# Moving the units' operand sums and steps to other slots in a one-core Strassen kernel on Trainium2

## The chip, the cores and the metric

The kernel runs on one core of one Trainium2 chip. A core has five engines, each with its own instruction queue: TensorE (PE in the profile, with its weight loads as PEld), VectorE (DVE), ScalarE (ACT), GpSimd (POOL) and SyncE (SP), which here only starts DMA transfers. Engines run at the same time and wait for each other by semaphores; within an engine instructions run strictly in the order of its queue. The metric is device time in microseconds (us) of one execution; the runs shown with it are repeated executions of the same kernel.

## The reference

```python
def reference(x, W1, b1, W2, b2, init_h, gate_w, sgate_w, sup_w, sdown_w, rgate_w, rup_w, rdown_w):
    xn = layernorm(x)                        # x: 8 x 1024 x 512, float32
    hidden, forget, inp = split(xn @ W1 + b1, 3)          # W1: 512 x 3072
    diff = softplus(-forget) - softplus(-inp)
    log_coeffs, log_values = -softplus(diff), -softplus(-diff) + log_g(hidden)
    out_h = scan over the 1024 positions, in log space, from log_g(init_h)
    s = out_h @ W2 + b2                      # W2: 1024 x 512
    shared = (silu(xn @ sgate_w) * (xn @ sup_w)) @ sdown_w     # 512 -> 1024 -> 512
    logits = xn @ gate_w                     # 32 experts, the best one is taken
    xs = xn * sigmoid(max(logits))
    routed = the same kind of layer with the weights of each token's own expert
    return x + s * silu(shared + routed)
```

All is in float32. There are 8192 tokens.

## The kernel before

**Two stages.** In the first (0 to some 2787 us of the profile) the recurrent layer and the shared expert are computed, the tokens' experts are chosen, and a table is built of which token goes where. In the second (2787 to 4124 us) the 32 routed experts run one after the other.

**Chunks, jobs and slots.** The first stage goes through 16 chunks of 512 tokens. A chunk has 20 *jobs*: blocks of the projections f, i, h (of W1), g and u (of the shared expert). A job is a product by Strassen's scheme: seven products of sums of quarters in place of eight products of quarters. Each product is one *slot* of PE work (`multiply`, matmuls on L925; ACT evicts the results on L939 and L941, VectorE and POOL join them on L951). So a chunk has SC = 140 slots; a slot is 1.21 us in the profile (169 to 170 us for a chunk).

**A hand-written order.** The kernel is emitted in the order in which the queues are to hold it. `now` counts slots. `at(slot, fn, ...)` puts a step into a slot. In each slot the loop at the end emits first the slot's product, then the steps that were put there, and then as many steps of the generator `project_out` (named `fill`) as `due(now)` asks for. No scheduler moves anything afterwards, but an engine reaches an instruction when its queue is done with those ahead of it, so that work put into slot 78 may run later, and never ahead of its place in the queue.

**Units.** What a chunk c produced is multiplied by the second matrix during chunk c+1, in two *units*: half 0 is the recurrent output times W2, half 1 the shared expert's product times sdown_w. A unit is again one Strassen product with seven banks, in the order P1, P2, P4, P6, P5, P3, P7. In chunks 1 to 13 a unit is "deep": each of the seven is itself done by Strassen's scheme, 49 steps in all. Steps of half 0 are due from slot 3 on and spread over 62 slots, those of half 1 over the 74 slots after. For each deep step there is a product of four matmuls (L1406), and for each bank:

- *outer sums* s1 to s4 of the unit's input (`out_combine`, L1275), four instructions of 128x256 each. s1 and s3 run on POOL, s2 and s4 on VectorE. There is one tile for each of s1 to s4, so a sum of the next unit overwrites that of this one and waits until PE has read it.
- *inner sums* of the quarters of those (`inner_sum`, L1388) on POOL;
- *inner evictions*: results are taken out of the accumulator bank by VectorE (L1415, the sum with a kept part; L1330, with the bias, for half 0) or ACT (L1324). A product waits for the eviction of the product before it in its bank.
- `out_add` (L1344) on VectorE, which adds the banks up, and then a store.

The weights of the steps come in pieces by DMAs that SP starts, four steps to a piece. Chunks 0, 14 and 15 are not deep: there the products of a bank are whole (L1461), and the bank of 128x512 is copied out by ACT (L1324), or by VectorE with the bias (L1330).

**The slots of the outer sums.** Half 0's sums of chunk c lie in slots 134 to 139 of chunk c and in slots 3 to 21 of chunk c+1 (q4 in 8 to 11, q3 in 18 to 21); half 1's in slots 62 to 85 of chunk c+1. For chunk 15 there are slots of their own ("fast").

**Ranks and table.** A step generator, `Dispatch.ranks`, counts for a quarter of the tokens how many before each chose the same expert. It runs one `yield` a slot (`spread_out`): VectorE makes one-hot rows and running sums, then it waits some slots, `aligned()` waits for the next group of seven slots, and two matmuls and a product and a sum on VectorE end it. It starts in slot 94 of chunks 2, 6 and 10. The fourth is the first part of `table()`, which starts in slot 77 of chunk 14 and goes on with `places` and `slots` (small VectorE operations on 128x64 tiles and 32-row columns, L1654 to L1691, and matmuls, L1606), `enter` (64 times, writes of rows to memory), `collect` and `merge`. The end of the table is the later of its own time and `END + 1`; both before and after, `END + 1` is the later.

**The tail.** After the last slot (END = 16 SC + 18) the rest of the last units runs alone, with the steps that are still open. In the sixth turn of that loop ACT starts the four DMAs of the first routed expert's first weights (`weight(0)`, `e_w`, L209); these stand in ACT's queue ahead of what is emitted later.

Of the kernel before, what the change touches and what calls it, by code (L numbers as in the profile page):

```python
# [34 lines left out]
def tile_kernel(  # L35
# [45 lines left out]
    nc = tc.nc  # L81
# [3 lines left out]
    E, _, I = rgate_w.shape  # L85
# [4 lines left out]
    NCHUNK = N // T  # L90
# [18 lines left out]
    def work(name):  # L109
        if now < SC:  # L110
            return pools["work"].tile([P, 512], FP, tag="w", name=name)
        assert now % 7 == 6
        return ps_x.tile([P, 512], FP, tag=f"x{(now // 7 + 1) % 2}", name=name)

    def aligned():
        while now % 7 != 6:
            yield
# [466 lines left out]
    def at(slot, what, *args):  # L584
        assert slot >= now
        steps.setdefault(slot, []).append(lambda: what(*args))
# [690 lines left out]
    for c in range(NCHUNK):  # L1277
        g = SC * (c + 1)
        fast = c == NCHUNK - 1
        for p in range(NP):  # L1280
            for q in range(1, 5):
                ends = p == NP - 1
                slot = {
                    1: 3 if ends else 134 + p - SC, 2: 6 if ends else 137 + p - SC,
                    4: 8 + p, 3: 13 + p // 2 if fast else 18 + p,
                }[q]
                at(g + slot, out_combine, c, 0, q, p)
                if fast:
                    slot = (24, 26, 31, 28)[q - 1] + p // 2
                else:  # L1290
                    slot = (62, 66, 82, 72)[q - 1] + p
                at(g + slot, out_combine, c, 1, q, p)

    def out_store(b, m, n):
# [25 lines left out]
    def out_copy(b, o, ps, first, n, reps=None):  # L1320

        c, half, name = ALL[b]
        if half or name not in ("P2", "P4", "P5"):
            nc.scalar.copy(o, ps)  # L1324
            return
        first += HC * (name == "P5")
        bias = b2b[:, first : first + n]
        if reps:
            bias = bias.unsqueeze(1).to_broadcast([P, reps, n])
        nc.vector.tensor_tensor(o, ps, bias, ALU.add)  # L1330
# [66 lines left out]
    def inner_product(step):  # L1397

        b, name = inner_of[step]
        if name == "P1":  # L1400
            out_bank[b] = out_bank_of(b)
        n = {"P2": 1, "P5": 2, "P3": 2}.get(name, 0)
        ps = out_bank[b][:, n * P : (n + 1) * P]
        w = out_w.pop(step)
        for i, lhs in enumerate(inner_lhs(b, name)):
            nc.tensor.matmul(  # L1406
                ps, lhsT=lhs, rhs=w[:, i, :], start=(name == "P1" and i == 0), stop=(i == 1),
                skip_group_check=True,
            )
        o = {"P2": (0, 0), "P3": (0, 1), "P4": (1, 0), "P7": (1, 1)}.get(name)  # L1410
        o = o and target(b)[:, o[0], o[1] * HQ : (o[1] + 1) * HQ]
        side = {"P2": "P1", "P3": "P6", "P7": "P5"}.get(name)
        if side:
            kept = inner.pop((b, side))
            nc.vector.tensor_tensor(o, ps, kept, ALU.add)  # L1415
        elif name == "P4":
            out_copy(b, o, ps, 0, HQ)
            at(now + 2, out_add, b)
        else:
            e = inner[b, name] = jp.tile(  # L1420
                [P, HQ], FP, tag="e" + name, name=f"e{name}_{b}", bufs=1 + (name == "P5")
            )
            out_copy(b, e, ps, 0 if name == "P1" else HQ, HQ)

    def project_out():
# [11 lines left out]
        for b, (c, half, name) in enumerate(ALL):  # L1437
# [14 lines left out]
            for q in range(2):  # L1452
                for p in range(NP):
# [17 lines left out]
                    if q == 1 and p == NP - 1:  # L1471
                        out_copy(
                            b, target(b), ps.rearrange("p (q f) -> p q f", q=2), 0, HC, 2
                        )
                        at(now + 1, out_add, b)
                        out_w.pop(("whole", b))
                        out_fetch()
                        if c == 0:
                            out_fetch()
# [8 lines left out]
    class Dispatch:  # L1488
# [16 lines left out]
        def ranks(self, q):  # L1505

            G = self.G
            q *= G
            oh = self.big([P, G, E], f"ohd{q}")
            nc.vector.tensor_tensor(  # L1510
                oh, self.bc(emax[:, q : q + G], E), self.rep(desc, G), ALU.is_equal
            )

            prev = self.big([P, G, E], f"prev{q}")
            yield
            if self.run is None:
                nc.vector.memset(prev[:, 0, :], 0.0)
            else:
                nc.vector.tensor_copy(prev[:, 0, :], self.run)
            for i in range(1, G):  # L1520
                nc.vector.tensor_tensor(
                    prev[:, i, :], prev[:, i - 1, :], oh[:, i - 1, :], ALU.add
                )
                if i % 4 == 3:
                    yield
            self.run = sm.tile([P, E], FP, name=f"run{q}", tag="run")
            nc.vector.tensor_tensor(self.run, prev[:, G - 1, :], oh[:, G - 1, :], ALU.add)
            for _ in range(9):
                yield
            yield from aligned()  # L1530
            ps = work(f"bef{q}")
            nc.tensor.matmul(
                ps, lhsT=upper, rhs=oh.rearrange("p t e -> p (t e)"), start=True, stop=False
            )
            nc.tensor.matmul(
                ps, lhsT=ones, rhs=prev.rearrange("p t e -> p (t e)"), start=False, stop=True
            )
            nc.vector.tensor_tensor(
                prev, ps.rearrange("p (t e) -> p t e", t=G), oh, ALU.mult
            )  # L1540
            yield
            nc.vector.tensor_reduce(rank[:, q : q + G], prev, AX.X, ALU.add)
            for _ in range(4):
                yield
            if q + G == NTILE:
                yield from aligned()
                self.totals = work("cps")
                nc.tensor.matmul(
                    self.totals[:, :E], lhsT=ones, rhs=self.run, start=True, stop=True
                )  # L1550
                nc.tensor.matmul(
                    self.totals[:E, E : E + 1], lhsT=self.run, rhs=ones[:, :1],
                    start=True, stop=True,
                )
# [267 lines left out]
    def due(slot):  # L1822

        c, s = divmod(slot, SC)
        if c == 0:
            return 0
        s -= 1
        before, (a, b) = sum(PER[: 2 * (c - 1)]), PER[2 * (c - 1) : 2 * c]
        if c == NCHUNK:
            return int(before + min(max(RATE * s, 0), a + b))  # L1830
        return int(before + min(max(s / 62, 0), 1) * a + min(max((s - 62) / 74, 0), 1) * b)
# [3 lines left out]
    for now in range(END):  # L1835
        job = now // 7
        name, back = ORDER[now % 7]
        if now < 7 * NPL:
            plain(job, now % 7)
        todo = (job - back,) if name != "P3" else (job - 1, job)  # L1840
        for n in todo:
            late = name == "P3" and n < JC
            if NPL <= n < NJOB and n == job - (1 if late else back):
                multiply(name, n)
        for step in steps.pop(now, ()):
            step()
        while filled < due(now):
            next(fill)
            filled += 1
# [21 lines left out]
    while filled < TOTAL:  # L1871
        now += 1
        for step in steps.pop(now, ()):
            step()
        while filled < due(now):
            next(fill)
            filled += 1
        k += 1
        if k in (6, 22):
            chunks[0].weight((0, "d")[k // 20], nc.scalar)  # L1880
        if filled >= TOTAL - 24 and "xsT" not in vars(chunks[0]):
            for t in range(CT):
                chunks[0].transpose(t)
# [143 lines left out]
```

## Time and profile before

| | us |
|---|---|
| runs | 4142.73, 4143.5, 4148.38 |
| median | 4143.5 |
| the profiled execution, its own time | 4148.08 |
| span of that execution | 4146.4 |
| mean granted clock of TensorE | 0.996 |

What PE did, and what stood ahead of the waits, by group of instructions in the profile:

| line, engine, what | count | busy us | idle before, us |
|---|---|---|---|
| L925 PE, the jobs' products (largest group) | 2536 | 654.6 | 11.1 |
| L1406 PE, deep steps from inner sums | 2912 | 445.5 | 22.2 |
| L1406 PEld, deep steps from outer sums | 1248 | 187.8 | 26.4 |
| L339 PE, the routed experts' second product | 2048 | 514.8 | 0.0 |
| L1388 POOL, inner sums of 128x256 | 208 | 221.1 | 99.8 |

How to read it: "busy" is the time of the group's instructions; "idle before" is the time in which their engine did nothing directly ahead of them, and the profile names what it takes to have ended that idle time, from the semaphores (the "releaser"). Where the named engine had long been done, it was another. Matmuls are pipelined, and PE is busy nearly everywhere: an idle stretch on PE is time lost, one on another engine is not unless PE waits for what comes late. The granted clock is the share of full speed at which PE was allowed to run.

The page divides the span into 40 slices. In the first 27 (the first stage) VectorE is busy 6 or 7 tenths and ACT 5 to 7; in the last 13 (the routed experts) PE is at 9 tenths of a slice or more and ACT at 2.

### The profile page before, as it was taken

The page shows a single profiled execution, that of the slowest core. Times are in us where ns is not written, and L with a number is a line of the kernel's source. Part 1 is how long each engine was busy: PE and PEld are TensorE (multiplying, and loading weights), DVE is VectorE, ACT ScalarE, POOL GpSimd, SP SyncE. Part 2 cuts the span into 40 slices and gives each one's busy share as a digit, 9 for nine tenths or more (in the row PEclk, how much of TensorE's full clock was granted, in tenths as well). Part 3 has the DMA queues.
Part 4 walks back from the last instruction along what each step waited for, and adds up shares of the span by engine and source line. Part 5 has one row for each costly group of instructions (what it writes and reads, how often), then busy time and mean ns, then how long its engine had stood idle before and what let it go on. Part 6 is the DMA issues. An engine that isn't in the chain of part 4 may idle for free. (4 is left out here: it accounts for less than half of the span.)

```text
span 4146.4 us, 70185 instructions
## 1 busy us (share of the span) xinstructions
PE 4059.2 (98%) x23699; PEld 3646.8 (88%) x23699; DVE 2642.8 (64%) x4489; ACT 2201.5 (53%) x4582; POOL 2254.1 (54%) x2603
## 2 busy tenths in 40 slices
PE   8999999999999999999999999999999999999997
PEld 6788889888888888988988888887899999999997
DVE  6766676676776766667676687444556656666631
ACT  5777766776667667676677765731222222222210
POOL 5445565555655655556655564634555555565542
PEclk9999999999999999999999999999999999999999
DMA  8788787787877778778777776666778788888884
GB/s 275 257 277 277 232 257 252 250 256 239 262 243 245 252 253 257 249 235 259 255 248 249 238 252 201 186 214 203 211 227 231 222 243 231 245 250 237 247 259 116
DMA packets 731387, 994.43 MB, mean 240 GB/s; under 512 B 75468, under 2 KB 523884, under 8 KB 730772
## 3 DMA queue, kind: packets, MB, share of 16 engines
q1 hardware_dynamic: 682020, 896.52, 67.8%
q0 software_dynamic: 46880, 89.20, 8.7%
q8 instruction: 193, 3.16, 0.3%
q10 hardware_dynamic: 2128, 4.19, 0.3%
q14 instruction: 166, 1.36, 0.1%
HBM read 858.39 MB, written 149.21 MB: 243 GB/s over the span
## 5 line engine op out<-in xcount | busy, mean ns | idle before, releaser
L925 PE MATMUL b<-t,sums 128*128 128x256 f32 x2536 | 654.6, 381 | 11.1 <-ACT u L939 5.2
L339 PE MATMUL acc<-e_h,e_wd 128*128 128x284 f32 (+26 forms) x2048 | 514.8, 394 | 0.0
L925 PEld LDWEIGHTS b<-t,sums 128*128 128x128 f32 x2536 | 455.4, 191 | 62.1 <-ACT u L939 7.3
L1406 PEld LDWEIGHTS u<-w_pieces,i 128*128 128x128 f32 x2912 | 435.7, 191 | 72.8 <-POOL i L1388 31.3
L1406 PE MATMUL u<-w_pieces,i 128*128 128x128 f32 x2912 | 445.5, 276 | 22.2 <-POOL i L1388 16.0
L339 PEld LDWEIGHTS acc<-e_h,e_wd 128*128 128x128 f32 x2048 | 373.8, 190 | 64.7
L260 POOL DMA_INDIRECT e_xs<-rec,fours x276 | 300.2, 1088 | 91.7 <-issue 88.6
L925 PE MATMUL b<-t,nat 128*128 128x256 f32 x1268 | 327.4, 381 | 4.7 <-ACT u L939 2.5
L925 PE MATMUL c<-t,sums 128*128 128x256 f32 x1268 | 328.3, 382 | 1.9 <-DVE lgT L694 1.5
L925 PE MATMUL c<-xnT,sums 128*128 128x256 f32 x1268 | 327.1, 381 | 2.4 <-ACT p L939 2.4
L925 PE MATMUL b<-xnT,nat 128*128 128x256 f32 x1268 | 327.5, 381 | 2.0 <-ACT i L941 2.0
L925 PE MATMUL a<-xnT,nat 128*128 128x256 f32 x1268 | 326.8, 380 | 0.0
L302 POOL COPY pin<-e_h 1x1 f32<-1x1 f32 x148 | 37.8, 255 | 479.3 <-DVE e_h L447 350.3
L1388 POOL TENSOR_TENSOR i<-s 128x256 f32<-128x256 f32 x208 | 221.1, 1065 | 99.8 <-PE u L1406 77.4
L941 ACT ACTIVATE u<-b,vec 128x256 f32<-128x256 f32 x378 | 180.5, 478 | 175.2 <-PE b L925 169.5
L925 PEld LDWEIGHTS b<-xnT,nat 128*128 128x128 f32 x1268 | 225.8, 191 | 37.4 <-DMA w_pieces<-d_P 7.8
L925 PEld LDWEIGHTS b<-t,nat 128*128 128x128 f32 x1268 | 228.0, 191 | 31.2 <-ACT u L941 4.2
L925 PEld LDWEIGHTS c<-t,sums 128*128 128x128 f32 x1268 | 225.6, 191 | 30.0 <-DVE lgT L694 7.2
L925 PEld LDWEIGHTS c<-xnT,sums 128*128 128x128 f32 x1268 | 226.8, 191 | 28.0 <-ACT p L939 4.9
L925 PEld LDWEIGHTS a<-xnT,nat 128*128 128x128 f32 x1268 | 226.7, 191 | 22.8
L1406 PEld LDWEIGHTS u<-w_pieces,s 128*128 128x128 f32 x1248 | 187.8, 191 | 26.4 <-DVE o L1415 10.1
L414 ACT COPY e_s<-e_b 128x284 f32<-128x284 f32 (+21 forms) x216 | 84.2, 390 | 237.3 <-PE e_b L405 237.3
(328 smaller groups left out, 9569.9 us busy)
## 6 DMA issues: line engine op xcount, KB each, us to landing
w_pieces<-d_P SPq DMA_DIRECT2D x1274, 128.0 KB, 3.2
sums<-sdram SPq DMA_DIRECT2D x300, 512.0 KB, 5.1
nat<-in_L_attn_W_dram SPq DMA_DIRECT2D x192, 512.0 KB, 4.7
e_w<-L_ffn_routed_gate_w_dram SPq DMA_DIRECT2D x126, 512.0 KB, 4.7
e_w<-n_L_ffn_routed_up_w_dram SPq DMA_DIRECT2D x126, 512.0 KB, 8.2
e_wd<-L_ffn_routed_down_w_dram SPq DMA_DIRECT2D x31, 2048.0 KB, 10.4
nat<-L_ffn_shared_gate_w_dram SPq DMA_DIRECT2D x64, 512.0 KB, 4.2
nat<-n_L_ffn_shared_up_w_dram SPq DMA_DIRECT2D x64, 512.0 KB, 4.2
```

The source lines that it names most:

```text
L260: nc.gpsimd.indirect_dma_start(out=self.xs[t][:, b, :], out_offset=None, in_=rec1.rearrange("n (a d) -> (n a) d", a=NA), in_offset=bass.In ...
L302: nc.gpsimd.tensor_copy(pin, self.mark)
L339: nc.tensor.matmul(accs[m][:, :W], lhsT=self.wd[:, j, m * P : (m + 1) * P], rhs=h[:, :W], start=(j == 0), stop=(j == NI - 1),)
L414: nc.scalar.copy(o[:, :W], ps[:, :W])
L925: nc.tensor.matmul(ps, lhsT=lhs[:, k, :], rhs=rhs[:, k, :], start=(new and k == 0), stop=(k == KQ - 1),  skip_group_check=True,)
L941: nc.scalar.activation(o, ps, AF.Identity, bias=bias(n, block))
L1388: nc.gpsimd.tensor_tensor(o, l, r, what)
L1406: nc.tensor.matmul(ps, lhsT=lhs, rhs=w[:, i, :], start=(name == "P1" and i == 0), stop=(i == 1), skip_group_check=True,)
```

## The change

Four edits, all of place and order but the last:

1. Half 1's outer sums of chunks 0 to 14: with p = 0 to 3, the slots of q1 (POOL) go from 62 + p to 68 + 2p, of q2 (VectorE) from 66 + p to 70 + 2p, of q3 (POOL) from 82 + p to 84 + 2p, and of q4 (VectorE) from 72 + p to 76 + 2p.
2. `due`: steps of the units begin two slots later in each chunk. All that a step emits goes along: products, inner sums, evictions, weight pieces, additions and stores. Half 0's outer sums stay in their slots.
3. `ranks`: the wait before its matmuls is 3 yields in place of 9, that at its end one in place of 4.
4. In the last unit (chunk 15, half 1) VectorE copies the banks out, not ACT.

```diff
@@ -1288,7 +1288,7 @@
                 if fast:
                     slot = (24, 26, 31, 28)[q - 1] + p // 2
                 else:
-                    slot = (62, 66, 82, 72)[q - 1] + p
+                    slot = (68, 70, 84, 76)[q - 1] + 2 * p
                 at(g + slot, out_combine, c, 1, q, p)
@@ -1321,7 +1321,10 @@
         c, half, name = ALL[b]
         if half or name not in ("P2", "P4", "P5"):
-            nc.scalar.copy(o, ps)
+            if c == NCHUNK - 1 and half:
+                nc.vector.tensor_copy(o, ps)
+            else:
+                nc.scalar.copy(o, ps)
             return
@@ -1525,7 +1528,7 @@
             nc.vector.tensor_tensor(self.run, prev[:, G - 1, :], oh[:, G - 1, :], ALU.add)
-            for _ in range(9):
+            for _ in range(3):
                 yield
             yield from aligned()
             ps = work(f"bef{q}")
@@ -1540,8 +1543,7 @@
             yield
             nc.vector.tensor_reduce(rank[:, q : q + G], prev, AX.X, ALU.add)
-            for _ in range(4):
-                yield
+            yield
             if q + G == NTILE:
                 yield from aligned()
@@ -1824,7 +1826,7 @@
         c, s = divmod(slot, SC)
         if c == 0:
             return 0
-        s -= 1
+        s -= 3
         before, (a, b) = sum(PER[: 2 * (c - 1)]), PER[2 * (c - 1) : 2 * c]
         if c == NCHUNK:
             return int(before + min(max(RATE * s, 0), a + b))
```

## The prediction

> **What bounds the kernel now.** I read the page first, then TensorE's waits by stretch, then timelines where the longest waits lie.
>
> ```profile
> span 4146.4 us, 70185 instructions
> PE 4059.2 (98%) x23699; PEld 3646.8 (88%) x23699; DVE 2642.8 (64%) x4489; ACT 2201.5 (53%) x4582; POOL 2254.1 (54%) x2603
> ```
>
> PE is busy 98% of the span. The change removes no matmul, so it can gain only what PE waits for, plus what PE loses at a low clock. The waits, first for the steady chunks (346 to 2381 us), then for the last chunks and the tail up to the routed experts (2381 to 2830):
>
> ```profile
> PE u L1406 <- POOL i L1388: 14.8, 13, 1.3
> PE u L1406 <- issue: 4.8, 12, 0.4
> PE u L1406 <- DVE o L1415: 2.5, 6, 0.4
> ...
> PE u L1406 <- DVE o L1415: 4.3, 2, 3.6
> PE u L1461 <- ACT T L1324: 1.7, 1, 1.7
> PE u L1406 <- POOL i L1388: 1.2, 1, 1.2
> PE u L1461 <- DVE h L1036: 1.1, 1, 1.1
> ```
>
> The columns are total us, times and longest. Units carry nearly all of it. Everything in these two answers, the 0.7 of the table's matmuls (L1606) and 0.4 of "issue" included, sums to 31.5 us. That caps the gain, clock aside.
>
> The largest row comes back once per chunk, every 169 to 170 us (438.50, 609.64, 778.66, ...): at 1.21 us per slot, slot 78 of 140. In chunk 4:
>
> ```profile
> 773.94 1.50 DVE L1072 TENSOR_TENSOR sh<-ssig,u 128x1024 f32<-128x1024 f32 x1
> 775.36 1.27 DVE L1275 TENSOR_TENSOR s<-sh,s 128x256 f32<-128x256 f32 x2
> 776.56 0.94 DVE L1344 TENSOR_TENSOR o<-o,o 128x512 f32<-128x512 f32 x1
> 777.53 0.83 DVE L1344 TENSOR_TENSOR o<-o,R 128x512 f32<-128x512 f32 x1
> 778.28 0.28 DVE L1415 TENSOR_TENSOR T<-u,eP 128x128 f32<-128x128 f32 x1
> 778.63 0.52 PEld L1406 LDWEIGHTS u<-w_pieces,i 128*128 128x128 f32 x4 [1.60 <-POOL i L1388]
> 778.66 0.68 PE L1406 MATMUL u<-w_pieces,i 128*128 128x128 f32 x4 [1.23 <-POOL i L1388]
> ```
>
> The profile blames POOL's inner sums (L1388), but POOL had made this product's operand long before. The product needs its bank, and the eviction `T<-u,eP` empties it at 778.56, 0.07 us before PE starts to load. Its own matmul ended near 772: the eviction stood six us in VectorE's queue. VectorE is the bound of this stretch alone:
>
> ```profile
> 764.00:780.00 16.00, 14.77 (x89) 12.02 (x87) 15.90 (x25) 7.51 (x20) 9.43 (x11) 1.00 0.66 217
> 780.00:796.00 16.00, 15.99 (x92) 14.35 (x92) 8.94 (x21) 14.16 (x28) 10.15 (x17) 1.00 0.89 280
> ...
> 2562.00:2564.00 2.00, 0.00 (x0) 0.00 (x0) 1.97 (x4) 0.00 (x0) 1.67 (x2) 0.81 0.06 23
> 2564.00:2566.00 2.00, 1.18 (x5) 1.18 (x6) 2.00 (x3) 0.00 (x0) 1.97 (x3) 0.50 0.01 0
> ```
>
> (Length; busy PE, PEld, DVE, ACT, POOL; granted clock.) DVE is busy 15.90 of 16.00 us, then 8.94. The two lower rows are the start of chunk 15, where PE stands 3.60 us and resumes at half clock.
>
> **The change, part by part.**
>
> *A: shared sums spread.* 16 sums of 128x256 per chunk, 15 chunks, no DMA. VectorE's q2 go from slots 66-69 to 70, 72, 74, 76, and q4 from 72-75 to 76-82; POOL's q1 from 62-65 to 68-74, q3 from 82-85 to 84-90. In the instruction order, six of the eight VectorE sums stood ahead of the late eviction; now three do. At 0.55 us each (4.53 us for eight in 764:780) three less are 1.7 us. *B: units two slots later* moves every PE step of the units, its inner sums, evictions and weight DMAs on SP by 2.42 us against sums and jobs, so PE asks 2.42 us later. Together 4.1 us of margin against waits of 1.0 to 1.3: all go. POOL's sums now run beside VectorE's, which costs something:
>
> ```profile
> L1275 DVE TENSOR_TENSOR s<-s,h x64: 390/416/951, 167.5 to 2739.2; 128x256 f32<-128x256 f32 x64
> L1275 DVE TENSOR_TENSOR s<-sh,s x64: 407/420/945, 265.5 to 2770.8; 128x256 f32<-128x256 f32 x64
> ```
>
> (min/median/max ns.) Alone 0.42, at worst 0.95: the three sums and two additions left ahead of the eviction could lose 0.5 each, 2.5 of the 4.1 us, and 1.6 still cover 1.3. I take -14.8-1.2 = **-16.0**; bounds -16.0 and -8.0 (half of the stretches stay late, or shift to another slot).
>
> This row speaks against A. [...] Taken as one engine at a time, four POOL sums of 0.72 would take 2.9 of the 4.1 us and leave about half of the waits: 4130 in place of 4122. The measured 0.95 shows the contention; no row here shows a full stop.
>
> B also acts at chunk starts: six waits of 0.42 at slot 8.6, behind evictions in VectorE's queue, against 2.42 us: **-2.5** (bounds -2.5, 0). The twelve 0.4 us "issue" waits are a late eviction too, at slot 40, where the whole unit moves with its evictions past other work: **0** (bounds -4.8, 0). Two half-0 sums (q4, slots 8-11) stay put and meet a tile that PE frees two slots later: rival R2. Here I take 0: VectorE ran the one at 863.86, and PE's read, ended by 861.71, moves to 864.1, so VectorE waits 0.3 at most. POOL's half-0 q1 sums (slots 134-136) wait two slots longer too, but the inner sums queued behind them are asked for two slots later: 0. SP's weight pieces (128 KB, 3.2 us to landing) keep their lead over the products, both moving together: 0.
>
> *C: shorter waits in the ranks.* Six and three yields less: the ranks' matmuls come a slot group earlier (chunk 2, 6, 10: slot 104), and the table's places, slots and row writes 7 slots, 8.5 us; the table's end is held by a fixed slot. The ranks' VectorE work was done in slot 101.7, so PE finds it ready: 0. In 2546 to 2561 VectorE is busy 14.59 of 15.00 us, some 7 us of it small table operations (L1654 to L1691); about 4.1 of them lie after 2550, just ahead of the late evictions. They leave; with B's 2.42 the margin is 6.5 us against 3.6 and 0.7 (2546.0): **-4.3**, and with the 3.6 goes the slow clock: 0.50 from 2564.8 to 2570, 5.2 us at half speed, **-2.6**. Bounds -6.9 and 0; the L1606 wait 0 (bounds -0.7, 0).
>
> *D: last unit's copies.* Seven 128x512 copies go from ACT (0.58) to VectorE (0.69 at L1330): seven times 0.11, in a stretch where each PE bank takes 3.4 us. They hide behind PE except the last: **+0.1** (bounds 0, +0.8).
>
> *E: the tail.* B's price. ACT issues expert 0's first weights at a fixed step, and was held there by a queue:
>
> ```profile
> 2755.16 0.58 ACT L1324 COPY o<-u 128x512 f32<-128x512 f32 x1 [6.32 <-PE u L1461]
> 2763.03 2.22 ACTq L209 DMA_DIRECT2D e_w<-L_ffn_routed_gate_w_dram  x2
> 2765.42 1.03 ACTq L209 DMA_DIRECT2D e_w<-n_L_ffn_routed_up_w_dram  x2
> 2766.55 0.58 ACT L1324 COPY T<-u 128x512 f32<-128x512 f32 x1 [10.81 <-DMA e_w<-L_ffn_routed_gate_w_dram]
> ```
>
> Behind these four issues stood one copy of half 0 (P7's bank), for which PE waited 1.71 us at 2767.19. With the unit five steps later two stand there, P3's and P7's. P3's bank is wanted eight steps earlier, eight times 0.43 us before 2765.5, so at 2762.0; its copy would end at 2765.1 (ACT freed 2 us sooner, as the table's DMAs go earlier) to 2767.1. PE waits 3.1 to 5.1 in place of 1.7: I take +2.1. D doesn't help: the copies that are held are half 0's, still ACT's. The 3.60 us row was followed by half clock, 2.6 us: +2.6. Two slots' later start ends the 1.10 us wait for the last scan at 2734.57: -1.1. **+3.6** (bounds -2.8, if ACT is freed in time, and +6.2, with 5.1 us and no gain at the scan).
>
> [...] This trace has the drop after 3.60 and nothing between that and 1.71.
>
> **Sum**: -16.0 -2.5 -4.3 -2.6 +0.1 +3.6 = -21.7, against the profiled 4148.1: 4126.4. That execution lies 4.6 above the runs' median, so 4143.5 - 21.7 = **4122**.
>
> **Rivals.**
> - *R1, the jam only moves.* For: DVE 15.90 of 16, POOL's sums now beside it, evictions' slack elsewhere only tenths. Against: 8.94 of 16 in the next stretch, where q4's tail now falls. Half of A, no B, half of the chunk 15 part: -8.0 - 3.4 + 3.6 + 0.1 = -7.7: 4136.
> - *R2, slower: half-0 sums collide.* They stay in their slots while PE frees their tile 2.42 us later. Where VectorE reaches q4 less than two slots late, it stands at the head of its queue until PE has read, up to 2.42 us, with evictions and job additions behind it, and PE waits for those. In 13 chunks 13 x 2.42 = +31: 4122 + 31 = 4153. For: at 863.86 against 864.1 there is no margin left, and whatever VectorE gains it waits. Against: VectorE is jammed from 848 to 868 whatever the shared sums do, and now never waits for PE there. It decides once VectorE catches up by more than the half us or so that evictions can be late.
> - *R3, the last chunks gain nothing.* The 3.6 us wait stays, since scans and additions of 1.2 to 1.8 us (L1036, L1072) stand right ahead of that eviction, and the tail is dear: -16.0 - 2.5 + 6.2 + 0.1 = -12.2: 4131.
> - *The change doesn't move what it says:* the table's end doesn't move, as said; nothing else is held so.
>
> **How the numbers follow.** 0.2% is 8.3 us, the least that this kernel's measurement tells from no change: 4135.2 to 4151.8 is "same". Forecast 0.60 (faster), R3 0.13 (faster), R1 0.15 (on the border; 0.14 same), R2 0.12 (slower). Faster 0.74, same 0.14, slower 0.12. Low end: all lower bounds, -16.0-2.5-4.8-6.9-0.7-2.8 = -33.7: 4110. High end: all upper bounds, -8.0+6.2+0.8 = -1.0: 4142.5, and a collision of 0.2 us in each of 13 chunks: 4145. R2's full price is left out.
>
> **What would show it.** A, B right: PE's wait on L1388 falls from 14 times to three or fewer, and DVE's busy time in slots 66 to 79 is clearly under 15.9 of 16. C: no idle over 1 us and no granted 0.50 at chunk 15's start. E: PE idle of 3 us or more near 2760 before L1461, ended by an ACT copy, two copies behind `e_w` issues. R2: idle over 1 us on DVE before L1275 with PE's L1406 as releaser, in most chunks. I am wrong if slot 78 still waits, if new waits of 0.3 us or more appear in most chunks elsewhere, or if the tail grows by more than 6 us.

## The result and the profile after

| | median, us | runs |
|---|---|---|
| before | 4143.5 | 7, from 4142.68 to 4148.38 |
| after | 4159.15 | 7, from 4158.43 to 4164.98 |

The changed kernel is slower: ratio 1.0037, 95% interval 1.0027 to 1.0047, or +15.65 us at the medians. 4122 had been forecast. The executions that are profiled from here on are each compared with the run that has VectorE's copies alone (4143.9 us in its profile, the same as before in its median), since the profiled execution of before was one of its slowest.

The page of the changed kernel:

```profile
span 4156.6 us, 70101 instructions
PE 4060.6 (98%) x23699; PEld 3650.5 (88%) x23699; DVE 2694.5 (65%) x4496; ACT 2204.5 (53%) x4575; POOL 2327.7 (56%) x2603
```

POOL has the same 2603 instructions as before and is busy 73.6 us longer. VectorE has seven more (the copies, 4.8 us) and is busy 51.7 us longer. So the same work takes both engines longer. The waits of TensorE, first the steady chunks (346 to 2381 us), then the last chunks and the tail (to 2830); line numbers are three higher after the inserted lines, so L1409 is the L1406 of before:

```profile
PE c L925 <- DVE lgT L694: 13.9, 12, 1.2
PE b L925 <- DVE t L837: 6.3, 6, 1.1
PE u L1409 <- DVE o L1418: 5.4, 11, 0.8
PE u L1409 <- POOL i L1391: 2.1, 6, 0.4
PE u L1409 <- POOL f L951: 1.8, 1, 1.8
...
PE u L1464 <- DMA w_whole<-tdram: 4.1, 1, 4.1
PE u L1464 <- ACT o L1327: 2.4, 1, 2.4
PE u L1409 <- DVE o L1418: 2.1, 2, 1.6
```

The waits of slot 78 and the 4.8 of "issue" are gone. In their place stand 13.9 us for `lgT`, the reduced logits of the router, once a chunk, and 11.7 us at the chunk starts, in the rows of `t` (L837, a sum of quarters of the chunk's input, which the jobs' products multiply) and of `o` (evictions). Chunk 4 at slots 76 to 80, the same place that the prediction showed of before:

```profile
775.82 1.21 DVE L1347 TENSOR_TENSOR o<-o,o 128x512 f32<-128x512 f32 x1
777.07 0.83 DVE L1347 TENSOR_TENSOR o<-o,R 128x512 f32<-128x512 f32 x1
778.41 0.28 DVE L1418 TENSOR_TENSOR T<-u,eP 128x128 f32<-128x128 f32 x1
778.61 0.67 DVE L694 TENSOR_REDUCE lgT<-lgt 128x128 f32<-128x512 f32 x1
779.34 0.92 PE L925 MATMUL c<-t,sums 128*128 128x256 f32 x3 [1.16 <-DVE lgT L694]
```

The late eviction `T<-u,eP` no longer holds PE. But right behind it in VectorE's queue stands the first reduction of the router's logits (L694). Its operand lies in the accumulator bank that the job's next product `c` needs, so PE waits 1.16 us there, at slot 79. The same two in the trace of before:

```profile
779.49 0.68 DVE L694 TENSOR_REDUCE lgT<-lgt 128x128 f32<-128x512 f32 x1
780.22 1.13 PE L925 MATMUL c<-t,sums 128*128 128x256 f32 x4
```

There the reduction ended at 780.17 and the product before `c` at 780.21, so PE lost nothing: the wait of 1.23 us just ahead, at slot 78, had covered this one.

By stage (starts of the same job's product in both traces, slot 25 of chunks 2, 14 and 15, and the start of the routed experts' second products):

| us | to chunk 2 | 12 chunks | chunks 14 to 15 | tail | rest |
|---|---|---|---|---|---|
| copies alone (as before) | 369.2 | 2036.0 | 180.6 | 211.3 | 1345.1 |
| after | 369.9 | 2044.1 | 177.3 | 220.2 | 1345.2 |

So +8.1 in the steady chunks, -3.3 in the last two, +8.9 in the tail. The first column varies by several us between runs of the same start (363 to 374 over all kernels here), and nothing is read from it.

### The profile page after: what moved, and what is told of

Read it like the earlier page. It is cut to its first block, busy times and chain, and to the rows that moved or that the text cites. A ratio compares the mean times of both kernels' runs of the same rounds, so it can differ in the third digit from the quotient of the medians.

```text
span 4156.6 us, 70101 instructions
## 1 busy us (share of the span) xinstructions
PE 4060.6 (98%) x23699; PEld 3650.5 (88%) x23699; DVE 2694.5 (65%) x4496; ACT 2204.5 (53%) x4575; POOL 2327.7 (56%) x2603
## 5 line engine op out<-in xcount | busy, mean ns | idle before, releaser
L1409 PEld LDWEIGHTS u<-w_pieces,i 128*128 128x128 f32 x2912 | 435.9, 191 | 58.8 <-POOL i L1391 10.9
L1409 PE MATMUL u<-w_pieces,i 128*128 128x128 f32 x2912 | 445.6, 276 | 6.1 <-POOL i L1391 2.1
L1275 POOL TENSOR_TENSOR s<-h 128x256 f32<-128x256 f32 x128 | 137.0, 1086 | 171.3 <-DVE h L1036 97.8
L1391 POOL TENSOR_TENSOR i<-s 128x256 f32<-128x256 f32 x208 | 188.1, 907 | 73.8 <-PE u L1409 71.2
L1409 PEld LDWEIGHTS u<-w_pieces,s 128*128 128x128 f32 x1248 | 186.2, 191 | 29.6 <-DVE o L1418 12.7
```

What stands on the lines that cost most here:

```text
L1275: eng.tensor_tensor(o, l, r, op_)
L1391: nc.gpsimd.tensor_tensor(o, l, r, what)
L1409: nc.tensor.matmul(ps, lhsT=lhs, rhs=w[:, i, :], start=(name == "P1" and i == 0), stop=(i == 1), skip_group_check=True,)
```

## The experiments

Differences are against the median of before that was measured with each kernel (4144.4 to 4145.8).

### Each part alone

The spread of the sums:

```diff
-                    slot = (62, 66, 82, 72)[q - 1] + p
+                    slot = (68, 70, 84, 76)[q - 1] + 2 * p
```

> Before with the spread of half 1's outer sums alone. Theory 1 (VectorE's jam has two deadlines, the eviction at slot 78 and the logits' first reduction at slot 79, and POOL's sums beside VectorE's take back most of what is moved away): PE still waits about 1.2 us at slot 78 in each chunk, the time is within 4 us of before (4143.5). Theory 2 (POOL's sums beside VectorE's are themselves the cost of the whole change): 8 to 15 us slower.

4143.08, **-1.4** (ratio 0.9996, interval 0.9987 to 1.0006). The wait of slot 78 stays; its row has 12.6 us in 13 waits against 14.8, and in chunk 4 it is 0.94 in place of 1.23. Theory 1.

The units two slots later, in `due`:

```diff
-        s -= 1
+        s -= 3
```

> Before with the units begun two slots later alone. Theory 1 (the later start brings the losses at the chunk starts, because half 0's sums stay in their slots and POOL stands longer ahead of them): PE waits at slots 9 to 13 of the chunks rise by about 1 us a chunk, the wait of slot 78 becomes one for the logits' reduction, chunk 15 keeps some 1.2 of its 3.6 us without the low clock; in the tail two copies behind the expert's weights, but no wait for a weight transfer: +4 to +14 us. Theory 2 (the sums' spread is the cost, the later start is gain): 0 to -8 us.

4163.06, **+18.6** (1.0027 to 1.0060). The 12 chunks take 2049.3 us, 13.3 more, and the tail 217.3, 6.0 more. PE's waits are 12.2 us for `lgT`, 6.3 for `t` and 9.5 for evictions and inner sums. This is theory 1, above its range: this edit alone loses more than the whole change.

The shorter waits in the ranks (the first yields 3 for 9, the last 1 for 4):

```diff
-            for _ in range(9):
+            for _ in range(3):
...
-            for _ in range(4):
-                yield
+            yield
```

> Before with the shorter waits in the ranks alone. Theory 1 (the table's small operations made chunk 15's eviction late; the tail is dear only where the table's transfer and the later weight transfers meet in SP's queue): -4 to -8 us, no PE wait over 1 us and no low clock at the start of chunk 15, no wait for a weight transfer over 1 us in the tail. Rival (the scans ahead of the eviction make it late, or the table's transfer blocks SP's queue by itself): 0 to +7 us.

4140.79, **-3.7** (0.9982 to 1.0001). Waits of PE in the last chunks fall from 3.6 and 0.7 to 1.1 and 0.2, and no transfer is waited for in the tail. This is theory 1's picture of the waits, the time a little short of its range; the interval just reaches no change.

VectorE's copies:

```diff
-            nc.scalar.copy(o, ps)
+            if c == NCHUNK - 1 and half:
+                nc.vector.tensor_copy(o, ps)
+            else:
+                nc.scalar.copy(o, ps)
```

> Before with the last unit's seven copies on VectorE alone. Both theories: within 1 us of before. Rival (VectorE's additions of half 0 stand ahead of the copies and PE waits for banks): +2 to +5 us in the tail.

4144.35, **-0.1** (0.9991 to 1.0010). As expected.

### POOL's sums beside VectorE's

The spread for VectorE's sums only; POOL's q1 and q3 stay at 62 to 65 and 82 to 85:

```diff
-                    slot = (62, 66, 82, 72)[q - 1] + p
+                    slot = (62 + p, 70 + 2 * p, 82 + p, 76 + 2 * p)[q - 1]
```

> Before, with VectorE's sums of half 1 spread as in the change (q2 70 to 76, q4 76 to 82) and POOL's left at their old slots (q1 62 to 65, q3 82 to 85). If POOL's sums beside VectorE's are what took the gain back: three sums of 0.55 less ahead of the eviction, PE's wait at slot 78 falls from 1.2 to below 0.3 us, 10 to 16 us less than before. If the spread sums would gain nothing anyhow: the wait stays at 0.9 to 1.2, within 3 us of before.

4121.68, **-22.8** (0.9929 to 0.9962), more than expected; no wait at slot 78 or 79 is left in the steady chunks. The only difference to the spread as a whole is where eight POOL instructions a chunk stand. VectorE runs the same list in the same order in both, so the timelines of chunk 4 can be laid side by side. First with the whole spread:

```profile
766.12 1.49 DVE L1068 TENSOR_TENSOR ssig<-ssig,g 128x1024 f32<-128x1024 f32 x1
767.54 0.67 DVE L1275 TENSOR_TENSOR s<-s,sh 128x256 f32<-128x256 f32 x1
768.13 0.67 DVE L951 TENSOR_TENSOR i<-c,u 128x256 f32<-128x256 f32 x1
768.73 0.28 DVE L1415 TENSOR_TENSOR R<-u,eP 128x128 f32<-128x128 f32 x1
768.93 1.55 DVE L1036 TENSOR_TENSOR_SCAN h<-i,ginit,f 128x512 f32<-128x512 f32 x1
...
774.60 0.28 DVE L1415 TENSOR_TENSOR T<-u,eP 128x128 f32<-128x128 f32 x1
```

and with POOL's sums left out of the stretch:

```profile
761.62 1.23 DVE L1068 TENSOR_TENSOR ssig<-ssig,g 128x1024 f32<-128x1024 f32 x1
762.76 0.42 DVE L1275 TENSOR_TENSOR s<-s,sh 128x256 f32<-128x256 f32 x1
763.10 0.42 DVE L951 TENSOR_TENSOR i<-c,u 128x256 f32<-128x256 f32 x1
763.43 0.28 DVE L1415 TENSOR_TENSOR R<-u,eP 128x128 f32<-128x128 f32 x1
763.63 1.27 DVE L1036 TENSOR_TENSOR_SCAN h<-i,ginit,f 128x512 f32<-128x512 f32 x1
...
768.75 0.28 DVE L1415 TENSOR_TENSOR T<-u,eP 128x128 f32<-128x128 f32 x1
```

From `ssig<-ssig,g` to the late eviction it is 8.48 us in the first and 7.13 in the second. Five instructions make the difference, the product (L1068), the sum, the addition (L951) and the scan shown and the product that follows (L1072, 1.50 against 1.22): each takes 0.25 to 0.28 us longer. The evictions, which read one operand from an accumulator bank, are 0.28 in both. The windows over these 11 us (length; busy PE, PEld, DVE, ACT, POOL) show POOL busy throughout in the first kernel:

```profile
764.00:775.00 11.00, 10.05 (x61) 8.67 (x57) 10.90 (x15) 4.74 (x12) 11.00 (x12) 1.00 0.60 199
```

and free for four of the 11 in the second, where VectorE gets three more instructions done; most of that is one gap ahead of a POOL addition, from 761.75 to 765.21, which is about where VectorE's five begin:

```profile
759.77:770.77 11.00, 11.00 (x68) 9.87 (x65) 10.86 (x18) 4.74 (x12) 6.96 (x10) 1.00 0.61 195
765.21 1.60 POOL L951 TENSOR_TENSOR i<-u,p 128x256 f32<-128x256 f32 x1 [3.46 <-ACT u L941]
```

After it POOL works in both kernels, and VectorE's instructions up to the eviction (the second sum 0.95, the unit's additions 0.94 and 0.83) take the same in both. VectorE's sums q2 read what POOL's q1 makes, so it might also have stood waiting for POOL; it didn't, being busy 10.90 of the 11.00 us.

The same in the changed kernel (POOL's half-1 sums back at their old slots, all else as changed):

> The changed kernel with POOL's half-1 sums back at their old slots (q1 62 to 65, q3 82 to 85); VectorE's spread, the later units, the shorter waits and the copies stay. If POOL's sums beside VectorE's cause the wait for the logits' reduction at slot 79 (1.16 us, 12 times): it goes, 4159.2 - 14 = 4145, the chunk starts and the tail stay as they are. If VectorE is late there anyhow: 4156 or more.

4140.87, **-4.2** against before (0.9980 to 0.9999), 18 below the changed kernel: the wait for `lgT` is gone, and the 12 chunks take 2029.4 in place of 2044.1. The chunk starts and the tail (220.4) are as they were. With POOL's sums where they had been, the change would have been faster than before.

### The later units

Half 0's and half 1's steps apart:

```diff
-        return int(before + min(max(s / 62, 0), 1) * a + min(max((s - 62) / 74, 0), 1) * b)
+        return int(before + min(max((s - 2) / 62, 0), 1) * a + min(max((s - 62) / 74, 0), 1) * b)
```

> Only half 0's steps begin two slots later, half 1's stay. Theory 1 (the chunk starts lose because half 1's last steps hold the tiles of half 0's sums two slots longer, so that POOL's sums run beside VectorE's): no loss from this part, within 4 us of before (4144.4), waits of slot 78 as before. Theory 2 (half 0's own steps and evictions fall into VectorE's jam at the chunk start): +8 to +16 us, with PE's waits at slots 9 to 13 as in the run with all units later.

4138.17, **-6.6** (0.9977 to 0.9996). Half 0's later start is a gain, which neither theory had.

> Only half 1's steps begin two slots later, half 0's stay. Theory 1: +8 to +16 us, PE's waits at slots 9 to 13 as in the run with all units later. Theory 2: within 4 us of before at the chunk starts. Both: the wait of slot 78 (1.2 us a chunk) becomes a wait for the logits' reduction at slot 79 of about 1 us.

(`(s - 64) / 74`, half 0 as it was.) 4178.99, **+34.3** (1.0066 to 1.0100). TensorE's waits in the steady chunks, of the kernel with half 0 later:

```profile
PE u L1406 <- POOL i L1388: 17.3, 17, 1.9
PE u L1406 <- DVE o L1415: 1.0, 6, 0.2
PE u L1406 <- issue: 0.7, 2, 0.4
```

and with half 1 later:

```profile
PE u L1406 <- DVE o L1415: 16.2, 11, 1.8
PE u L1406 <- POOL i L1388: 14.4, 13, 1.3
PE c L925 <- DVE lgT L694: 11.9, 12, 1.0
PE u L1406 <- issue: 5.0, 13, 0.4
```

In the first the "issue" waits of slot 40 are gone. In the second the evictions of half 1's last banks, which now come two slots further into the next chunk, cost 0.6 to 1.8 us in every chunk from the third on at slot 9 in place of 0.4 in every other one. Against the expectation the waits of the L1388 row, nearly all near slot 78, stay as well (14.4 us) beside the new ones for `lgT` (11.9). So the loss is theory 1's half, half 1, and larger than expected. The halves don't add up, though: over the 12 chunks -8.9 and +30.8 against +13.3 for both together. A likely reason, not tested: with half 1 alone later, half 0's first products ask for their banks two slots sooner after those evictions than with both later.

What do those evictions stand behind? All of half 0's sums two slots later, with the units:

> All units two slots later, and half 0's outer sums two slots later with them. Theory 1: the sums keep their distance to the steps but still run late among VectorE's additions; some of the loss goes, +5 to +12 us in place of +18.6. Theory 2 (the steps meet VectorE's jam, wherever the sums are): +15 us or more.

4152.50, **+7.8** (1.0008 to 1.0027), as theory 1 had it. And VectorE's half-0 sums alone moved behind the chunk start, POOL's left:

```diff
-                    1: 3 if ends else 134 + p - SC, 2: 6 if ends else 137 + p - SC,
-                    4: 8 + p, 3: 13 + p // 2 if fast else 18 + p,
+                    1: 3 if ends else 134 + p - SC,
+                    2: (6 if ends else 137 + p - SC) if fast else 22 + p,
+                    4: 8 + p if fast else 26 + p, 3: 13 + p // 2 if fast else 18 + p,
```

> All units two slots later, and VectorE's half-0 sums behind the chunk start (q2 22 to 25, q4 26 to 29); POOL's stay. If VectorE's sums ahead of the late evictions are the loss at the chunk starts: PE's waits at slots 9 to 13 go, 10 to 14 us less than the later units alone (4163), 4149 to 4153. If POOL's held sums, or the jobs' scans, are the loss: 4158 or more.

4137.44, **-7.1** (0.9975 to 0.9994), 25.6 below the later units alone; twice what was expected. This run is called b_q24 below. Its waits in the steady chunks:

```profile
PE c L925 <- DVE lgT L694: 12.3, 12, 1.0
PE u L1407 <- POOL i L1389: 2.5, 8, 0.3
PE u L1407 <- issue: 1.3, 4, 0.3
```

The rows of slots 9 to 13 for `t` and `o` are gone, and `lgT` is left. So the chunk starts lose because VectorE's eight half-0 sums stand in front of half 1's late evictions and of `t`, not because POOL's are held.

### The tail

The timeline of SP's queue in the changed kernel, where PE waits until 2749.66 for a weight transfer:

```profile
2744.99 0.33 SPq L1733 DMA_DIRECT2D table<-two  x1
2745.41 0.86 SPq L1214 DMA_DIRECT2D w_whole<-tdram  x2
```

`table<-two` writes the merged table and waits for VectorE's last merge, which ends at 2744.96. In the order of before these two weight transfers stand ahead of it:

```profile
2737.74 3.92 SPq L1214 DMA_DIRECT2D w_whole<-tdram  x2
2744.79 0.38 SPq L1211 DMA_DIRECT2D w_whole<-in_L_attn_W_dram  x1
2747.78 0.33 SPq L1731 DMA_DIRECT2D table<-two  x1
```

The ranks' shorter waits move it seven slots up, the later units move the transfers two slots down, and together they change places. The later units alone have no such wait for `w_whole<-tdram`; there `table<-two` has got ahead of the third transfer only (`w_whole<-in_L_attn_W_dram`), for which PE waits 2.1 us. The shorter waits alone have neither wait. What follows is at half clock (windows, last but two the granted clock):

```profile
2748.00:2750.00 2.00, 0.34 (x1) 0.37 (x2) 2.00 (x4) 0.00 (x0) 0.00 (x0) 0.65 1.00 390
2750.00:2752.00 2.00, 2.00 (x6) 1.54 (x6) 0.90 (x1) 0.00 (x0) 0.00 (x0) 0.50 1.01 355
2752.00:2754.00 2.00, 2.00 (x6) 1.59 (x5) 0.00 (x0) 0.00 (x0) 0.00 (x0) 0.50 0.06 19
```

Table and expert's weights back at their old distance to the units:

```diff
-        at(end + 13 + which, d.merge, which)
+        at(end + 20 + which, d.merge, which)
...
-        if k in (6, 22):
+        if k in (8, 22):
```

> The changed kernel with the table's merges seven slots later and the first expert's weights two slots later, both at their old distance to the units. Theory (the changed tail loses 9 us because the table's transfer stands ahead of two weight transfers in SP's queue, and because two copies of half 0 stand behind ACT's four weight issues): no wait for a weight transfer near 2749, a wait of under 2 us in place of 2.36 for the copies, no stretch at half clock; 4159.2 less 7 and less 2 to 5: 4147 to 4150. Rival (half 0's later start is late by itself): 4155 or more.

4154.01, 5.1 below the changed kernel and +8.2 against before (1.0012 to 1.0031). The tail falls from 220.2 to 212.3, near the 211.3 of the unchanged order, and the wait for the copies is gone. The total gained less than expected, between theory and rival: PE still waits 2.2 us for one weight transfer, the same one as with the later units alone and again issued right behind `table<-two`.

The changed kernel without the later units:

> The changed kernel with the units back at their old slots (sums spread, shorter waits, VectorE's copies stay). If the later units are the whole loss and the rest adds up: 4144.6 - 1.4 - 3.7 - 0.1, 4139 to 4140, faster than before. Rival (the table's transfer, seven slots earlier, is dear in the tail without the later units too): 4145 or more.

4142.67, **-3.2** (0.9984 to 1.0003), between the two cases; the interval reaches no change. The gains of the parts don't quite add up, and the tail takes 212.9.

### Versions that take the jam apart

Half 1's sums behind the jam, with the ranks' shorter waits:

```diff
-                    slot = (62, 66, 82, 72)[q - 1] + p
+                    slot = (80, 82, 98, 90)[q - 1] + 2 * p
```

> Units as before; the ranks' shorter waits, and half 1's outer sums not spread but behind VectorE's jam: q1 in slots 80 to 86, q2 82 to 88, q4 90 to 96, q3 98 to 104. If the jam of slots 66 to 79 with its two deadlines is what PE waits for, both waits go: 13 waits of 1.2 us less, with the ranks' 3.7 us together -15 to -22 us against 4144.4. Rival (the evictions stand behind scans and products of the jobs, not behind sums): -3 to -8 us, the wait of slot 78 stays.

4122.59, **-22.1** (0.9931 to 0.9964): the two waits go, as the theory has it. A new one of 1.55 us comes at slot 104 of chunks 2, 6 and 10, where the ranks' running sums now meet q4. So q4 goes ahead of those, and half 0's later steps (the first edit under "The later units") come in:

```diff
-                    slot = (62, 66, 82, 72)[q - 1] + p
+                    slot = (80, 82, 96, 86)[q - 1] + p
```

> Shorter waits in the ranks; half 1's outer sums behind the jam and ahead of the ranks' running sums (q1 80 to 83, q2 82 to 85, q4 86 to 89, q3 96 to 99); half 0's steps alone two slots later. If the gains are separate: 4144.6 - 22 (late sums with the ranks) - 4 (three waits of 1.55 at slot 104) - 6.5 (half 0 later) = 4112. If they overlap: 4116 to 4123.

4110.54, **-35.3** (0.9900 to 0.9933): the gains are separate. This run is called best1 below. On top of it all of half 0's sums behind the chunk start:

```diff
+                    1: (3 if ends else 134 + p - SC) if fast else 14 + p,
+                    2: (6 if ends else 137 + p - SC) if fast else 22 + p,
+                    4: 8 + p if fast else 26 + p, 3: 13 + p // 2 if fast else 34 + p,
```

> As the run beside it, with half 0's outer sums, too, behind the chunk starts' jam (q1 14 to 17, q2 22 to 25, q4 26 to 29, q3 34 to 37). If sums in the jam at the chunk starts make evictions late there as they do at slot 78: the waits at slots 8 to 13 go, 3 to 8 us less than the run beside it, 4104 to 4109. If not: the same within 2 us.

4124.80, **-21.0** (0.9938 to 0.9971), a miss: the chunk starts' waits go, but 12 waits of 1.6 us for POOL's inner sums come near slot 42, behind the slots that POOL's q3 was moved to (34 to 37). Last, VectorE's half-0 sums alone behind the chunk start (best1 with the two lines for q2 and q4 of b_q24 above):

> The fastest run so far (late sums of half 1, shorter waits in the ranks, half 0's steps two slots later; 4110.5) with VectorE's half-0 sums behind the chunk start as well. If these sums make the last waits at slots 10 to 13: 3 to 6 us less, 4104 to 4108. Rival (VectorE's sums in slots 22 to 29 stand ahead of half 0's evictions there): 4113 or more.

4102.32, **-42.2**, ratio 0.9897 (0.9880 to 0.9913), a little more than expected. This run, best3, is the fastest version here, faster than both kernels. With POOL's half-0 sums back in place the waits near slot 42 are gone, too. All that TensorE waits for in the steady chunks:

```profile
PE u L1407 <- DVE o L1416: 0.4, 2, 0.2
PE u L1407 <- POOL i L1389: 0.4, 1, 0.4
```

## Why the prediction was wrong

**What it had right.** The bound: PE's waits in the units, and behind them VectorE's queue rather than the POOL that the profile named. In all 13 waits of slot 78 before, the late eviction ended 0.10 us ahead of PE's product, and best3 gains mostly by moving sums out of VectorE's two jams, with not a matmul less. Edit C: the chunk 15 wait fell from 3.6 us to 1.1 alone and 1.6 in the whole change. In the whole change the low clock behind it is gone as well (granted 1.00 throughout from 2548 to 2574), but that 2.6 can't be put down to the edit: with the copies alone a wait of 3.38 us stays there without it (below). D: nothing. In E, two half-0 copies behind the four weight issues, a wait of 2.36 (3.1 to 5.1 forecast) and a slow stretch after it (granted 0.62 and 0.53 in the windows from 2772 to 2776).

**A, the step that failed.** "The three sums and two additions left ahead of the eviction could lose 0.5 each, 2.5 of the 4.1 us, and 1.6 still cover 1.3." Two things are wrong in it. The contention was charged to those five instructions, sums and the unit's additions, but the scans, the products and the jobs' additions pay too: in chunk 4, 1.1 of the 1.35 us lie on them. With the spread alone, PE's wait for the eviction in chunk 4 fell only from 1.23 to 0.94 us, with three sums less ahead of it. And the price was put into a margin for one deadline. A second, the reduction at slot 79, hung on the same queue a few instructions on with no margin but the first wait itself, and PE's new wait there is 1.16; the later units alone, with the sums in their old slots, already show it (12.2 us). The forecast -16.0 became nothing. One of its 13 waits in the steady chunks, 1.26 us, lies at the start of chunk 2, not at slot 78; with the one of chunk 14, slot 78 had 14.8 us in 13 waits, and slot 79 now has 15.1 in 13. The mechanism was rival R1's, "the jam only moves", at a chance of 0.15; R1 still forecast a gain, and the sign came from the other terms.

What the contention takes stands in the traces of the two spreads, in chunk 4: five VectorE instructions took 0.25 to 0.28 us longer with POOL busy for 11.00 of 11 us than with POOL busy for 6.96, and the evictions, with one operand in an accumulator bank, kept 0.28 us. The forecast had weighed the contention and then priced too few instructions.

**B, chunk starts.** Forecast -2.5 ("six waits of 0.42 ... against 2.42 us"); the waits there rose instead, from 2.5 us to 6.3 for `t` and 5.4 for `o`. Half 0's later start alone gains; it is half 1's, which moves that half's last evictions further into the next chunk's jam, that loses. The working looked at what comes earlier than the moved steps, not at what they run into. VectorE's half-0 sums, left in place, are in the way (b_q24), which is near R2's place, but not its mechanism: VectorE doesn't stand waiting for PE (in the steady chunks none of its sums does; they wait for POOL alone, 3.1 us in all), its queue is simply full there (busy 21.89 of 22 us from 850 to 872 in the changed kernel). "Issue", taken as 0, gave its 4.8.

**E, the tail.** Forecast +3.6, measured +8.9. The step: "SP's weight pieces keep their lead over the products, both moving together: 0." Pieces and products do move together, but the table's write in the same queue doesn't move with them: B alone puts it ahead of one transfer (2.1 us), and C, which moves it up, ahead of two more. The two edits were summed one by one. The missing term is the 4.1 us wait with 2.9 of slow clock behind it (granted 0.50 from 2749.66 to 2754 and 0.65 in the next 2 us). (The upper bound of +6.2 is mis-added, too: 5.1 - 1.7 + 2.6 is 6.0.)

**The sum.** -21.7 forecast; the profiles give +14.4 against the run with the copies alone: +8.1 in the steady chunks, -3.3, +8.9 and 0.7 at the start. Two of the prediction's own signs of being wrong came true: new waits of more than 0.3 us in most chunks, and a tail longer by more than 6 us.

## What to carry to other kernels

When an engine's queue is the bound of a stretch, list every deadline that hangs on it there, not only the one that shows: the next may have no margin, hidden by the first. Work of a second engine that is moved into that stretch can cost as much as is moved out, as POOL's did VectorE here (4143.08 us with POOL's sums moved along, 4121.68 without), so move it to where the first engine is idle. Edits that shift two things in one in-order queue have to be laid over each other before they are summed.

## What was not expected of the hardware

How much POOL's work slows VectorE's: eight POOL sums of 0.7 us a chunk, in other slots, made 21.4 us of difference (4143.08 against 4121.68; 17.3 of it, by the profiles, in the 12 steady chunks) without an instruction more or less on either engine.

Here the low clock doesn't follow from the length of one idle stretch. With VectorE's copies alone PE stood idle for 3.38 us up to 2562.93 and went on at full clock:

```profile
2560.00:2562.00 2.00, 0.00 (x0) 0.00 (x0) 1.97 (x4) 0.07 (x1) 1.56 (x2) 1.00 0.03 12
2562.00:2564.00 2.00, 1.07 (x7) 1.02 (x8) 2.00 (x4) 0.27 (x1) 1.97 (x3) 1.00 0.01 0
```

In best1, 1.92 us up to 351.91 were followed by half clock:

```profile
350.00:352.00 2.00, 0.09 (x1) 0.12 (x2) 2.00 (x5) 1.04 (x2) 2.00 (x3) 1.00 1.09 387
352.00:354.00 2.00, 2.00 (x9) 1.72 (x10) 2.00 (x4) 0.27 (x2) 2.00 (x5) 0.70 1.74 722
354.00:356.00 2.00, 2.00 (x7) 1.62 (x7) 1.66 (x2) 0.67 (x2) 2.00 (x3) 0.50 0.08 35
```

In the changed kernel's tail 2.36 us were followed by 0.62 and 0.53 (2772 to 2776). So 2.36 and 1.92 us were followed by a low clock and 3.38 was not. The prediction's "nothing between that and 1.71" holds for the last chunks and the tail, not for the whole trace of before: 2.79 us up to 72.12 were followed by 0.50 (72 to 78), and 2.80 up to 10.00, 1.98 up to 64.81 and 1.84 up to 95.70 by 1.00. What PE did in the microseconds around the gap was not tried.
